# Attention and a bottleneck convolution on one core: the first output projection by quarters, weight parts prepared across the first batch, and three moved steps

## The chip, the cores and the metric

The kernel runs on one core of one Trainium2 chip. The metric is the device time of one execution in microseconds (us); lower is better. A profiled execution gives a span on the core, from its first to its last instruction, and a trace of every instruction on every engine.

## The reference, cut to what matters

Everything is float32. Four batches of a 1024 x 1024 token matrix pass through an attention layer and then a bottleneck convolution with batch norms over all four batches:

```python
B, C, H, W = hidden_states.shape          # 4, 1024, 32, 32
x = hidden_states.reshape(B, C, N).transpose(0, 2, 1)          # N = 1024 tokens
qkv = (x @ w_qkv.T + b_qkv).reshape(B, N, 3, nh, hd)            # 16 heads of 64
q, k, v = (qkv[:, :, 0], qkv[:, :, 1], qkv[:, :, 2])
q = _apply_rope(q, cos, sin); k = _apply_rope(k, cos, sin)
q = _rmsnorm(q.reshape(B, N, inner), q_norm_w); k = _rmsnorm(k..., k_norm_w)   # norm over all heads
attn = softmax(q k^T * hd ** -0.5)
out = _rmsnorm((attn v) @ w_proj.T, norm_out_w) + residual
...
out = relu(bn(conv1x1(x, w1)))            # 1024 -> 256 channels
out = relu(bn(conv3x3(out, w2)))          # 256 -> 256
out = bn(conv1x1(out, w3))                # 256 -> 1024
out = relu(x + softplus(residual_scale) * out)
```

## The kernel before, in words

**Stages.** The batches b = 0 to 3 are a Python loop (L958). Each has three projections, `q`, `k` and `v`, then attention in two halves c of the tokens with eight pairs of heads hp in each (`attention`, L753), then the output projection `y`. After the loop come the first convolution (`conv1`), the second (by tiles in a transformed domain, `uv`, L1166) and the third. All instructions of TensorE, VectorE, ScalarE and GpSimd (POOL) keep the order in which the Python code issues them; the loads on SyncE's queue (SP) are put in order by the framework.

**Projections by halves and by quarters.** A projection multiplies a 1024 x 1024 weight by 1024 x 1024 data with fewer products than the eight that the 2 x 2 blocks need. `project` (L290) does it *by halves*, one level: seven block products, each in four groups of output channels g, so 28 products of four matmuls of 512 columns. `project2` (L435) does it *by quarters*, two levels: seven outer parts k of seven products each, 49 products of four matmuls of 256 columns. The profile counts each float32 matmul as two instructions. Before the change batch 0 goes by halves and batches 1 to 3 by quarters.

**Weight parts.** By quarters, a weight of an outer part is needed as seven pieces: three are read as they are (m = 0, 1, 6), and four are sums that `prepare` (L400) makes once: four loads of 256 KB, four additions on VectorE (L407 to L410), four writes by POOL into the DRAM array `wd2` (L412). Such a group I call a *part*; there are seven per weight, 28 in all. Parts k = 2 to 5 are made from the one-level sums in `wd`, which batch 0's `project` makes itself in `operands` (L224: four loads, four additions L236 to L239, four writes L242, for each g). Where parts are made: in the attention of batch 0, one per pair of heads (`extra_step`, L989), the seven of q, the seven of v and one of k; in y of batch 0, by a delayed step (L1040), the other six of k; in the attention of batch 1 the seven of the output weight WP.

**Delayed steps.** `after(n, step)` (L254) puts a step n units later, a unit being one product by halves or two by quarters. `waiting` holds steps with a cost in units (`TT` per VectorE operation of 512 columns); `product_done` (L257) lets them out as the room allows. The rotation of q and k (`rope`, L699) is such a step for each of eight tiles: two VectorE operations of 1024 columns and two accumulating DMAs by POOL. After the last tile SP loads the tables of angles anew (`load_tables`, L168), which the norms had been multiplied into.

**Buffers.** Weights pass through a ring of eight 256 KB buffers (`wring`, L157), which parts made in attention use too. Parts in y of batch 0 use three larger ones (`big`). The tile of k and y (`kp`) and the room `v_room` are one buffer each, used in turn. PSUM has four banks `o1` and four `o2` during projections; the sums of a norm (`inverse_rms`, L674) take one of `o2`.

**Around y of batch 0.** The inverse denominators of the last pairs are computed at its start (`inverses`, L812) and copied by SP (L817, L822); `mean_of_v` (L747) multiplies by them and adds a bias on POOL (L751); the sums of data for the products (L281 to L284) follow.

**Around the second convolution.** `other_channels` (L1143) fills the padded tile of batch 0 (`fill`, L1097: a relu on ScalarE), VectorE makes differences of it (L1109), and then `fill(1, 1)` overwrites the tile with batch 1. `copies` (L1180) takes two banks from PSUM on ScalarE, after which TensorE goes on in them.

Of the kernel before, what the change touches and what calls it, by code (L numbers as in the profile page):

```python
# [11 lines left out]
F32 = mybir.dt.float32  # L12
AF = mybir.ActivationFunctionType
ALU = mybir.AluOpType
# [71 lines left out]
def program(ctx, tc, x, wblk, w2, w3, vecs, cos, sin, out, bad):  # L86
# [66 lines left out]
    with tc.tile_pool(name=f"st{u}", bufs=2) as st, ExitStack() as s:  # L153
# [14 lines left out]
        def load_tables():  # L168
            nc.sync.dma_start(cosT, cos)
            for i in range(2):  # L170

                nc.sync.dma_start(sinT[i::2, :], sin[1 - i :: 2, :])
# [25 lines left out]
        def bank(kind, name):  # L198
            pool, shape = psum[kind]
            return pool.tile(shape, F32, tag=kind, name=name)  # L200
# [43 lines left out]

        TT = 0.21
        later, waiting = [], deque()
        pace = {"at": 0, "room": 0.0, "hold": False}

        def spend(cost):
            pace["room"] -= cost
# [1 line left out]
        def after(n, step):  # L254
            later.append((pace["at"] + n, step))
# [144 lines left out]
        def prepare(which, base, k, alloc, queue=nc.sync):  # L400

            a11, a12, a21, a22 = a = alloc(f"pre_{which}_{k}")
            for i, t in enumerate(a):
                quarter(t, base, k, i // 2, i % 2, queue)

            def make():
                nc.vector.tensor_tensor(a22, a21, a22, ALU.add)  # L407
                nc.vector.tensor_tensor(a21, a11, a21, ALU.subtract)
                nc.vector.tensor_tensor(a11, a22, a11, ALU.subtract)
                nc.vector.tensor_tensor(a12, a12, a11, ALU.subtract)  # L410
                for m, t in enumerate((a11, a22, a21, a12)):
                    nc.gpsimd.dma_start(wd2[which, k, m], t)  # L412

            return make

# [246 lines left out]
        def beside(bs, ts, units, odd):  # L662


            def room(k):
                at = 8 + 4 * ((k + odd) % 2)
                return units[at : at + 4]

            def spare(k, oq, tq):
                return units[2 * (k % 2)] if (oq, tq) == (0, 1) else units[4 + 2 * oq]  # L670

            return operand(bs, ts), room, spare

        def inverse_rms(total, eps, scale, name, then):  # L674


            r = temp(f"rms_{name}")[:, :QT]
            row = inv_d[norms_done.pop(0)]

            def root():  # L680
                o = bank("o2", f"ss_{name}")[:, :QT]
                for q in range(4):
                    nc.tensor.matmul(
                        o[q * QH : (q + 1) * QH, :], ones[:, :QH], total[:, q * QT : (q + 1) * QT],
                        start=True, stop=True,
                    )
                nc.scalar.activation(r, o, AF.Sqrt, bias=eps, scale=scale)
                after(0.5, invert)

            def invert():  # L690
                spend(3 * TT)
                nc.vector.reciprocal(r, r)
                nc.gpsimd.dma_start(row.rearrange("(q t) -> q t", q=4), r[::QH, :])
                nc.gpsimd.dma_start(total, row.partition_broadcast(P))
                after(2.5, then)

            after(4, root)

        def rope(b, dst, total, eps, scale, w, tag, biased=True):  # L699

            def tables():
                for t in (sinT, cosT):
                    nc.vector.tensor_tensor(t, t, total, ALU.mult)

            def turn(f):
                k, other = dst[:, f, :], big_temp(f"{tag}s_{b}_{f}")
                for i, (t, table) in enumerate(((other, sinT), (k, cosT))):
                    if w is not None:  # L710
                        nc.vector.scalar_tensor_tensor(t, k, w[i][:, f : f + 1], table, ALU.mult, ALU.mult)
                    elif biased:
                        nc.vector.tensor_tensor(t, k, table, ALU.mult)
                    else:
                        nc.vector.scalar_tensor_tensor(t, k, col("bq", f), table, ALU.add, ALU.mult)
                for i in range(2):
                    nc.gpsimd.dma_start(dst[i::2, f, :], other[1 - i :: 2, :], accum_op=ALU.add)  # L717
                if f == NT - 1 and (b, tag) != (B - 1, "k"):
                    load_tables()

            def then():
                waiting.append((4 * TT, tables))
                for f in range(NT):
                    waiting.append((4 * TT, lambda f=f: turn(f)))

            inverse_rms(total, eps, scale, f"{tag}_{b}", then)
# [211 lines left out]
        def units_of(room):  # L938

            units = [flat(room[:, i // 2 : i // 2 + 1, :])[:, half[i % 2]] for i in range(16)]  # L940
            return [t.rearrange("p (q e) -> p q e", q=2) for t in units]

        vector_and_act = {mybir.EngineType.DVE, mybir.EngineType.Activation}
        regions = ExitStack()
        regions.enter_context(tc.manual_schedule(engines=vector_and_act))
# [12 lines left out]
        for b in range(B):  # L958
# [3 lines left out]
            if b > 0:  # L962
                two2 = [beside(xs[b], ts[b], units, odd) for odd in (1, 0)]
                two2.append(in_place(xs[b], ts[b], room, True))
                ahead.append(two2[1][:2])
            two = (0, *two2[0], b == 1) if b > 0 else None
            tq = qk_proj(b, WQ, xs[b], ts[b], "bq", q_all, "q", w1 if b == 0 else None, two, True)
            rope(b, q_all, tq, eps_q, HD / C, None, "q", b == 0)
            k_all = kp.tile([P, NT, N], F32, tag="k", name=f"k_{b}")
            if b > 0:  # L970
                ahead.append(two2[2][:2])
            two = (3, *two2[1], False) if b > 0 else None
            tk = qk_proj(b, WK, xs[b], ts[b], "bk", k_all, "k", None, two)
            rope(b, k_all, tk, eps_rms, 1.0 / C, (wqk_other, wqk), "k")
            v = room
# [4 lines left out]

            todo = []
            if b == 0:
                todo = [(which, base, k) for which, base in ((0, WQ), (1, WV)) for k in range(len(OUTER))]
                todo.append((3, WK, 0))
            elif b == 1:
                todo = [(2, WP, k) for k in range(len(OUTER))]
            made = []

            def extra_step():  # L989
                if made:  # L990
                    made.pop()()
                if todo:
                    made.append(prepare(*todo.pop(0), pieces))

            extra = [extra_step] * (len(todo) + 1) if todo else []
            if b == B - 1:
                extra = filters()
            if b > 0:
# [22 lines left out]
            if b + 1 < B:  # L1021
                xs[b + 1] = x_tile(b + 1)
                ts[b + 1] = t_tiles(b + 1)
                rows = (0, 1, 4, 5, 2, 3, 6, 7)
                for j in range(NT):

                    def load(b=b, i=rows[j]):
                        for c in range(NCH):
                            load_x(b + 1, c, (i,))

                    after(3 + 1.5 * j, load)
                for i in range(0, NH, 2):

                    def queue(b=b, i=i):
                        waiting.append((7 * TT, lambda: sums(ts[b + 1], xs[b + 1], i)))

                    after(3 + 1.5 * (2 * i + 3) + 2, queue)
                if b == 0:
                    for k in range(1, len(OUTER)):
                        after(5 * k - 4.5, lambda k=k: after(4, prepare(3, WK, k, big_pieces, nc.gpsimd)))  # L1040
            else:
                back = {1: x_tile(b + 1)}
                for i in range(NT):
                    after(8 + 1.5 * i, lambda i=i: read_back(1, (i,)))
            yt[b] = kp.tile([P, NT, N], F32, tag="k", name=f"y_{b}")
            two = None
            if b > 0:
                two = (2, *in_place(q_all, tc_, yt[b], False), True)
                if b + 1 < B:
                    ahead.append(beside(xs[b + 1], ts[b + 1], units_of(room), 1)[:2])  # L1050
            ty = qk_proj(b, WP, q_all, tc_, None, yt[b], "y", None, two)
            if b + 1 < B:
                o_norm(b, ty, yt[b])
# [89 lines left out]
        def other_channels():  # L1143
            norm1(1)
            fill(0, 1)
            for j in (1, 2, 0, 3):
                across(1, j)
                for r in range(2):
                    down(0, 1, r, j)
            for r in range(2, 4):  # L1150
                down(0, 1, r)
            fill(1, 1)

        for b in range(2):
            load_h1(b)
# [87 lines left out]
        for b in range(B):  # L1243
# [8 lines left out]
            for f in range(NPT):  # L1252
                for h in range(2):
                    if b > 0:
                        start_banks(b, f, h)
                        uv(b, f, h, 0, 0)
                    uv(b, f, h, 0, 1)
                    copies(b, f, h)
                    for i in range(NPT):
                        uv(b, f, h, 1, i)  # L1260
                    if due:
                        outputs(*due)
                    due = (b, f, h)
                    for step in steps[:4]:
                        step()
                    steps = steps[4:]
# [138 lines left out]
```

## Time and profile before

| | us |
|---|---|
| median of 3 runs (2730.69 to 2731.75) | 2731.07 |
| profiled execution | 2734.88 |
| its span | 2733.0 |
| TensorE (PE) busy | 2692.9 |
| VectorE (DVE) busy | 2091.9 |
| ScalarE (ACT) busy | 1081.1 |
| GpSimd (POOL) busy | 403.3 |

The page is that of the profiled execution, so parts of it add up to its own span of 2733.0 and not to the median. Matmuls are pipelined: the start of one group of them to the start of the next is the time that a group takes, while the "us" of a group has its drain in it. In lines of the timeline the first two numbers are the start and the duration, and a bracket at the end gives idle time ahead of the group and what ended it. Two numbers beside an engine in a table of windows are the busy time and the count of instructions.

### The profile page before, as it was taken

Reading aid. Unit: us, or ns where it says so; the run is one execution under the profiler, and the core shown is the slowest. Engines: PE = TensorE matmul, PEld = TensorE weight load, DVE = VectorE, ACT = ScalarE, POOL = GpSimd, SP = SyncE. Lnnn points to the kernel's source line nnn. Section 1 sums busy time; section 2 is a strip of 40 time slices with the busy share of each in tenths; the row PEclk is TensorE's granted clock in tenths of the full one; section 3 lists DMA queues with packets and bytes.
Section 4 is the critical chain, followed back from the end, with each engine's and each line's share of the span. In section 5 each row is a group of like instructions: output and inputs, shape, how many; then the busy total and the mean of one; then the engine's idle time right before and its main releaser. Section 6 shows DMA issues by size and latency. Waiting matters only on the chain.

```text
span 2733.0 us, 32908 instructions
## 1 busy us (share of the span) xinstructions
PE 2692.9 (99%) x11746; PEld 1652.8 (60%) x11746; DVE 2091.9 (77%) x2406; ACT 1081.1 (40%) x1494; POOL 403.3 (15%) x471
## 2 busy tenths in 40 slices
PE   9999999999999999999999999999999999999997
PEld 4449633347888433588886333888884335846843
DVE  4355599966788889888888877887888878646987
ACT  2221455413342555333343555233525653312266
POOL 1033022332011232100112100100112201000000
PEclk9999999999999999999999999999999999999999
DMA  5376255587668645356667410665687103662165
GB/s 208 105 189 185 89 156 158 179 276 251 189 181 216 139 122 156 117 168 220 178 191 186 89 24 16 200 195 183 181 238 148 25 23 125 198 240 85 62 221 211
DMA packets 238252, 432.05 MB, mean 158 GB/s; under 512 B 27072, under 2 KB 116464, under 8 KB 238080
## 3 DMA queue, kind: packets, MB, share of 16 engines
q1 hardware_dynamic: 202784, 312.30, 36.4%
q0 software_dynamic: 35296, 117.56, 16.7%
q8 instruction: 96, 1.57, 0.2%
q14 instruction: 76, 0.62, 0.1%
HBM read 295.22 MB, written 96.78 MB: 143 GB/s over the span
## 4 chain that ended last, share of the span: by engine, by line
PE 92%; DMA 3%; DVE 2%; ACT 2%; issue 0%; SPq 0%; POOL 0%; ACTq 0%; POOLq 0%; DVEq 0%
PE sc L770 17%; PE cx L787 16%; PE p_q L461 9%; PE p_y L461 9%; PE p_v L456 8%; PE p_k L461 7%; PE c L859 4%; PE c L1309 4%; PE pa_q L304 2%; PE pa_v L312 2%; PE pa_k L304 2%; PE c2x L1170 2%; PE c2y L1170 2%; DMA w_v<-wdf 2%; PE pa_y L304 2%; PE dn L808 1%
## 5 line engine op out<-in xcount | busy, mean ns | idle before, releaser
L781 DVE TENSOR_TENSOR den<-den,p 128x1024 f32<-128x1024 f32 x384 | 470.5, 1225 | 41.1 <-DVE den L781 0.9
L777 ACT ACTIVATE p<-sc 128x1024 f32<-128x1024 f32 x512 | 476.2, 1043 | 55.6 <-PE sc L770 55.6
L770 PE MATMUL sc<-q,k 64*128 64x512 f32 x2048 | 457.1, 596 | 3.0 <-DVE to L482 2.3
L770 PEld LDWEIGHTS sc<-q,k 64*128 64x128 f32 x2048 | 191.2, 186 | 266.8 <-issue 121.5
L787 PE MATMUL cx<-p,to 128*64 128x512 f32 x1536 | 340.2, 595 | 0.0
L787 PEld LDWEIGHTS cx<-p,to 128*64 128x64 f32 x1536 | 106.0, 137 | 228.3 <-issue 228.3
L751 POOL TENSOR_SCALAR q<-q,vec 128x512 f32<-128x512 f32 x64 | 130.7, 2049 | 524.6 <-DVE q L750 514.3
L792 ACT COPY q<-cx 128x512 f32<-128x512 f32 x64 | 37.6, 587 | 357.3 <-PE cx L787 357.3
L456 PE MATMUL p_v<-w_v,x 128*128 128x256 f32 x696 | 157.9, 379 | 1.9 <-DMA w_v<-wdf 1.9
L461 PE MATMUL p_y<-q,w_y 128*128 128x256 f32 x696 | 157.5, 380 | 0.0
L461 PE MATMUL p_k<-to,w_k 128*128 128x256 f32 x672 | 153.1, 381 | 2.3 <-ACT k L549 1.5
L461 PE MATMUL p_q<-to,w_q 128*128 128x256 f32 x672 | 152.5, 380 | 0.1
L456 PEld LDWEIGHTS p_v<-w_v,x 128*128 128x128 f32 x696 | 132.0, 190 | 21.0 <-DMA w_v<-wdf 3.1
L461 PEld LDWEIGHTS p_y<-q,w_y 128*128 128x128 f32 x696 | 131.8, 190 | 20.7 <-issue 2.5
L461 PEld LDWEIGHTS p_k<-to,w_k 128*128 128x128 f32 x672 | 126.7, 190 | 23.5 <-ACT to L549 2.8
L461 PEld LDWEIGHTS p_q<-to,w_q 128*128 128x128 f32 x672 | 127.2, 190 | 19.5 <-issue 1.6
L779 DVE TENSOR_TENSOR den<-p 128x1024 f32<-128x1024 f32 x64 | 76.5, 1196 | 76.6 <-ACT p L777 76.6
L814 DVE RECIPROCAL rec<-dn 128x512 f32<-128x512 f32 x32 | 107.2, 3350 | 14.1 <-PE dn L808 14.0
L787 PE MATMUL cx<-p,rq 128*64 128x512 f32 x512 | 113.4, 595 | 0.0
L1309 PE MATMUL c<-h,w 128*128 128x512 f32 x256 | 110.3, 592 | 0.9 <-ACT h L1213 0.9
L717 POOL DMA_DIRECT2D q<-qs x64 | 55.6, 1020 | 289.6 <-issue 190.8
L717 POOL DMA_DIRECT2D k<-ks x64 | 55.2, 997 | 242.1 <-ACT p L777 91.1
(521 smaller groups left out, 4271.9 us busy)
## 6 DMA issues: line engine op xcount, KB each, us to landing
wd2f<-w_pre POOLq DMA_DIRECT2D x88, 256.0 KB, 2.9
w_q<-wd2f SPq DMA_DIRECT2D x84, 256.0 KB
w_k<-wd2f SPq DMA_DIRECT2D x84, 256.0 KB
w_v<-wd2f SPq DMA_DIRECT2D x84, 256.0 KB
w_y<-wd2f SPq DMA_DIRECT2D x84, 256.0 KB
x<-in_x_dram SPq DMA_DIRECT2D x64, 256.0 KB
q<-qs POOLq DMA_DIRECT2D x64, 256.0 KB, 5.4
k<-ks POOLq DMA_DIRECT2D x64, 256.0 KB, 5.4
```

What stands on the lines that cost most here:

```text
L304: nc.tensor.matmul(o, w[:, i, :], r(i), start=first and i == 0, stop=last and i == NH - 1, skip_group_check=True,)
L456: nc.tensor.matmul(o[:, q].rearrange("p (g f) -> p g f", g=2), r[:, i, q * P : (q + 1) * P], wt[:, :, i, :], skip_group_check=True, **at,)
L461: nc.tensor.matmul(o[:, q], wt[:, q, i, :], r[:, i, :], skip_group_check=True, **at)
L717: nc.gpsimd.dma_start(dst[i::2, f, :], other[1 - i :: 2, :], accum_op=ALU.add)
L751: nc.gpsimd.tensor_scalar(cx, cx, col("bv", hp), None, ALU.add)
L770: nc.tensor.matmul(sc[:, j], k_all[d, hp, t * P : (t + 1) * P], q_all[d, hp, at], start=True, stop=bad is not None,)
L777: nc.scalar.activation(p, sc, AF.Exp)
L781: nc.vector.tensor_tensor(d_, d_, p, ALU.add)
L787: nc.tensor.matmul(o[j * HD : (j + 1) * HD, :], v[:, t, h0 : h0 + HD], probs[t][:, j], start=(t == 0), stop=(t == N // P - 1),)
L859: nc.tensor.matmul(o, w[f][ih][:, ii, :], ys[:, i, half[c]], start=(i == 0), stop=(i == NT - 1))
L1170: nc.tensor.matmul(o[:, r * TR * TC : (r + 1) * TR * TC], uw[2 * h + r, j][:, i * PL + f * P : i * PL + (f + 1) * P], vt[b, i][:, 2 * h + ...
L1309: nc.tensor.matmul(os[i], w3t[k][f // NH][:, f % NH, :], h2[b, k][:, half[c]], start=(k == 0), stop=(k == NPT - 1),)
```

## The change

Line numbers below are those of the kernel before.

- The output projection of batch 0 goes through `project2`, as those of later batches. Its one-level sums of WP are made by a new `prepare_blocks` in the attention of batch 0, and the sums ahead for q of batch 1 are made at its end.
- Parts are spread anew. Seven (three of q, three of v, one of k) are made in q of batch 0, in a tile of `kp` that k takes later; five (four of q, one of k) in k of batch 0, in `room`, which v takes later; both are loaded by POOL. In the attention of batch 0: four blocks of WP, its seven parts, and five of k, the loads of the first being issued ahead of the attention. Four of v are made in y of batch 0 (the last one ends in q of batch 1). None are left in the attention of batch 1.
- The rotation of k waits until 2.5 units after the tables of angles are loaded (`pace["tables"]`).
- The sums of the norms take a bank of `o1` rather than `o2`, but for q and k of batch 0.
- `TT` goes from 0.21 to 0.19.
- `fill(1, 1)` is issued after the first `copies`.

```diff
-        TT = 0.21
+        TT = 0.19
...
+        def prepare_blocks(base, g, alloc, queue=nc.sync):
+            a11, a12, a21, a22 = a = alloc(f"blk_{base}_{g}")
+            for i, t in enumerate(a):
+                ih = i % 2
+                queue.dma_start(t, wblk[base + g + NG * (i // 2)][:, ih * NH * P : (ih + 1) * NH * P])
+            def make():
+                nc.vector.tensor_tensor(a22, a21, a22, ALU.add)
+                nc.vector.tensor_tensor(a21, a11, a21, ALU.subtract)
+                nc.vector.tensor_tensor(a11, a22, a11, ALU.subtract)
+                nc.vector.tensor_tensor(a12, a12, a11, ALU.subtract)
+                for o, t in enumerate((a11, a22, a21, a12)):
+                    nc.gpsimd.dma_start(wd[base // NT * NG + g, o], t)
+            return make
...
-                o = bank("o2", f"ss_{name}")[:, :QT]
+                o = bank("o2" if name in ("q_0", "k_0") else "o1", f"ss_{name}")[:, :QT]
...
                     load_tables()
+                    pace["tables"] = pace["at"] + 2.5
...
             def then():
+                if pace["at"] < pace["tables"]:
+                    after(pace["tables"] - pace["at"], then)
+                    return
...
+        def weight_parts(parts, first, step, lag, alloc):
+            for i, (which, base, k) in enumerate(parts):
+                def begin(which=which, base=base, k=k):
+                    after(lag, prepare(which, base, k, alloc, nc.gpsimd))
+                after(first + i * step, begin)
...
-            two = (0, *two2[0], b == 1) if b > 0 else None
+            two = (0, *two2[0], False) if b > 0 else None
+            if b == 0:
+                unused = kp.tile([P, NT, N], F32, tag="k", name="unused")
+                parts = [(which, base, k) for which, base in ((0, WQ), (1, WV)) for k in (0, 1, 6)]
+                parts.append((3, WK, 0))
+                weight_parts(parts, 8, 2.7, 2.5, pieces_of(unused))
...
+            if b == 0:
+                parts = [(0, WQ, k) for k in (2, 3, 4, 5)] + [(3, WK, 1)]
+                weight_parts(parts, 2, 4.5, 2.5, pieces_of(room))
...
             if b == 0:
-                todo = [(which, base, k) for which, base in ((0, WQ), (1, WV)) for k in range(len(OUTER))]
-                todo.append((3, WK, 0))
-            elif b == 1:
-                todo = [(2, WP, k) for k in range(len(OUTER))]
+                todo = [lambda g=g: prepare_blocks(WP, g, pieces) for g in range(NG)]
+                todo += [
+                    lambda which=which, base=base, k=k: prepare(which, base, k, pieces)
+                    for which, base, ks in ((2, WP, (0, 1, 6, 2, 3, 4, 5)), (3, WK, (2, 3, 4, 5, 6)))
+                    for k in ks
+                ]
...
-                    for k in range(1, len(OUTER)):
-                        after(5 * k - 4.5, lambda k=k: after(4, prepare(3, WK, k, big_pieces, nc.gpsimd)))
+                    weight_parts([(1, WV, k) for k in (2, 3, 4, 5)], 6, 7, 4, big_pieces)
...
-            two = None
-            if b > 0:
-                two = (2, *in_place(q_all, tc_, yt[b], False), True)
-                if b + 1 < B:
-                    ahead.append(beside(xs[b + 1], ts[b + 1], units_of(room), 1)[:2])
+            two = (2, *in_place(q_all, tc_, yt[b], False), True)
+            if b + 1 < B:
+                ahead.append(beside(xs[b + 1], ts[b + 1], units_of(room), 1)[:2])
...
             for r in range(2, 4):
                 down(0, 1, r)
-            fill(1, 1)
...
                     copies(b, f, h)
+                    if (b, f, h) == (0, 0, 0):
+                        fill(1, 1)
```

`pieces_of(tile)` hands out quarters of a tile's sixteen 512-column pieces in turn; `extra_step` is called once ahead of the attention, so that the first loads are under way.

More of the change, by code (lines that the diff above doesn't have):

```diff
@@ L243, in operands @@
             return [a11, s1, a21, a12, a22]
-        TT = 0.21
+        TT = 0.19
         later, waiting = [], deque()
-        pace = {"at": 0, "room": 0.0, "hold": False}
+        pace = {"at": 0, "room": 0.0, "hold": False, "tables": 0.0}
         def spend(cost):
@@ L941, in units_of, with pieces_of, alloc @@
             return [t.rearrange("p (q e) -> p q e", q=2) for t in units]
+        def weight_parts(parts, first, step, lag, alloc):
[3 more added lines that the diff above has]
+                after(first + i * step, begin)
+        def pieces_of(tile):
+            at = deque(tile[:, i, h] for i in range(NT) for h in half)
+            def alloc(name):
+                at.rotate(-4)
+                return [at[i] for i in range(-4, 0)]
+            return alloc
         vector_and_act = {mybir.EngineType.DVE, mybir.EngineType.Activation}
@@ L992, in extra_step @@
                 if todo:
-                    made.append(prepare(*todo.pop(0), pieces))
-            extra = [extra_step] * (len(todo) + 1) if todo else []
+                    made.append(todo.pop(0)())
+            extra = [extra_step] * len(todo)
+            if todo:
+                extra_step()
             if b == B - 1:
```

## The prediction

> **What bounds the kernel now.** I read the busy times first, then the chain that ended last, then TensorE's waits, then the timelines of the stretches that the change touches.
>
> ```profile
> PE 2692.9 (99%) x11746; PEld 1652.8 (60%) x11746; DVE 2091.9 (77%) x2406; ACT 1081.1 (40%) x1494; POOL 403.3 (15%) x471
> PE 92%; DMA 3%; DVE 2%; ACT 2%; issue 0%; SPq 0%; POOL 0%; ACTq 0%; POOLq 0%; DVEq 0%
> ```
>
> TensorE is busy 99% and is 92% of the chain. Only fewer matmuls, or fewer waits of TensorE, can pay; work moved among the others costs nothing until TensorE waits for it. I call a projection by its letter and batch: q_0 is 5.4 to 103.8 us, k_0 to 200.7, v_0 to 301.7, the attention of batch 0 to 535.7, y_0 (output projection) to 639.4. Now TensorE in y_0, and after it the windows of q_0, k_0, y_0, y_1:
>
> ```profile
> 549.51 13.90 PE L304 MATMUL pb_y<-q,w_y 128*128 128x512 f32 x32
> 567.19 6.54 PE L304 MATMUL pa_y<-to,w_y_0b 128*128 128x512 f32 x8 [3.78 <-issue]
> 573.57 3.60 PE L304 MATMUL pc_y<-to,w_y_0b_s 128*128 128x512 f32 x8
> 577.00 3.60 PE L304 MATMUL pa_y<-q,w_y_0b 128*128 128x512 f32 x8
> ```
>
> ```profile
> 5.40:103.80 98.40, 98.37 (x225) 43.46 (x226) 37.92 (x62) 20.95 (x35) 8.56 (x16) 1.00 0.49 172
> 103.80:200.70 96.90, 96.90 (x234) 42.63 (x233) 51.08 (x61) 23.38 (x38) 23.97 (x34) 1.00 0.61 168
> 535.70:639.40 103.70, 99.59 (x228) 43.48 (x225) 63.67 (x81) 18.73 (x32) 43.46 (x66) 0.97 0.78 263
> 1133.50:1218.00 84.50, 84.50 (x391) 73.96 (x392) 75.09 (x93) 25.64 (x45) 6.34 (x4) 1.00 0.66 203
> ```
>
> (Columns: stretch, length, busy us of PE, PEld, DVE, ACT, POOL, clock, share of the DMA engines, GB/s.) A product by halves is 8 matmul instructions, 3.43 us apart. y_0 has 28: 96.1 us, but it takes 103.8, and one line shows where most of the 7.6 us go: 3.78 idle for late operands, then 6.54 us for a product instead of 3.60. y_1 is the same projection by quarters: 49 products at 1.727 us, 84.6 us, with no wait in it. Last, what y_0 starts behind (POOL writes a prepared part, SP loads weights), and the late wait in the convolution:
>
> ```profile
> 537.88 2.18 POOL L412 DMA_DIRECT2D wd2f<-w_pre  x4
> 540.32 3.85 SPq L221 DMA_DIRECT2D w_y<-in_wblk_dram  x4
> 543.84 7.46 DMA w_y<-in_wblk_dram
> 2499.46 1.25 ACT L1098 ACTIVATE pad<-h1l,sh,sc 128x1024 f32<-128x1024 f32 x1 [5.14 <-DVE cols L1109]
> 2501.22 1.83 PE L1170 MATMUL c2x<-V,t_w 128*128 128x256 f32 x4 [2.39 <-ACT c2x L1185]
> ```
>
> **What the Trainium skill says.** "TensorE: Matmul & The Clock Gate", Part 1: The HAM clock gate: after an idle window of about 3.4 us the array runs at half rate until it has been busy for about as long. The trace agrees: +2.9 us after 3.78 idle; and 2.39 idle at 2501 costs nearly as much (1.83 and 1.91 for runs of 1.03). So I price a TensorE wait of 2 us or more at itself plus 2 to 3. The same page, Architectural detail: VectorE is a strict FIFO. The trace agrees: from 545.5 to 552.4 VectorE sits before L750 for a DMA, and the first addition of pb_y, whose product ends at 553, comes at 563.8 behind it. "DMA: Bandwidth & Descriptors", Queues, rings and completion order: a DMA engine takes packets of its queues in turn. So parts loaded by POOL do not block SP's weights, but share the bandwidth; the trace shows 7.46 us for a 256 KB load at 543.84, where the parts' writes take 2.9.
>
> **The change part by part.** Durations are of the profiled execution, 2734.88 us with a span of 2733.0; it stands 3.8 above the median of 2731.07, and I take the difference off the median.
>
> (a) y_0 by quarters: 103.8 to 85.0 (y_1's stretch from first matmul to q_2's). **-18.8**: 11.5 is arithmetic, the rest y_0's present waits.
>
> (b) The new start of y_0. All weights pass through a ring of 8 buffers. The last part of the attention holds four; VectorE adds it up at 534 to 537.5, POOL writes it at 537.9 to 540.1, behind its two bias additions, and the buffers come free from 540.3 to 543.8, as SP's four w_y loads show. By halves the four buffers are wanted at 549.5 (A12). By quarters the fifth product (the start of the second of seven outer parts) is due at 535.7 + 4 x 1.727 = 542.6, and its weight is the eighth of the ring, fourth behind that release: issued at about 544.5, in about 4 us later, with 1 MB in the burst. TensorE waits about 5.5 and restarts at half rate, 2.5: **+8**, ends +2 (loads in 2 us, no half rate) and +12 (7.46 us again). Behind it on SP stand the x8 copies of the inverse denominators, so the last means of v and the second sums end near 558, as now (L282 at 557.6); they are wanted by the 14th product, 558.1 plus this wait. No second wait there.
>
> (c) The rest of y_0. VectorE as in y_1, 75.1, plus three of v's four parts at 4 x 0.69 = 2.8: 83.5 of some 94 us, and its first sums start 3 us later against TensorE than y_1's (537.5 for 535.7, 1131.8 for 1133.4). DMA: 17.2 MB as in y_1 plus three parts of 2.1 MB; at the 0.337 MB/us that y_0 has now (27.3 MB in 0.78 x 103.7) 74 of 94 us. Both fit, tightly: **+1.5**, ends 0 and +6.
>
> (d) k_0 gets five parts, q_0 seven, all loaded by POOL: per part 4 loads of 0.72 us on POOL, 4 additions on VectorE, 4 writes of 0.54. q_0: VectorE 37.9 + 19.6 = 57.5 of 98.4; DMA in 35 to 70 us 0.41 plus 3.6 parts at 6.2 us: full. But operands are done there 8 us before use (61.5 for 69.5): **+0.5**, ends 0 and +4. k_0 is the narrow one: from 132 to 166 VectorE is busy 29.8 of 34 us with q's rotation, DMA 0.83; two parts add 5.6 and 12.4. The operands of group 2 (L238) end at 161.3 now and are wanted at 166.4. The written order puts two parts and one more turn (2.4) before them and about 3 us of idle time is there to absorb it: 161.3 + 8 - 3 = 166.3, if no part is late. But POOL issues the second part's loads behind writes that wait for VectorE (about 151), 6 to 8 us before they land. Queued behind VectorE's wait are those operands, and SP's last piece of group 3 waits for the tables, thus for the turn: it is in at 179 now, wanted at 183.5. **+3**, ends 0 and +9.
>
> (e) Attention 0 has 16 parts for 15 (four are WP's operand sums, that y_0 made itself); attention 1 loses seven. 0: VectorE 210.6 + 2.8 of 233.4, and no wait of TensorE there names it or a DMA.
>
> (f) The relu (1.25 us) behind the copies: they no longer stand behind it and VectorE's columns (2499.4). TensorE's products end at 2498.8, so copy and go on at about 2499.6 instead of 2501.2: 1.6, and its slow restart (1.8): **-3.2**, ends -1 and -4.
>
> (g) TT, tables, banks: in the written order seven of q's turns, not five, precede k's norm in batches 1 to 3, and six of k's, not four, the attention. VectorE in a k stage rises from 70.3 to 75.5 of 86.8, y_1's share, which TensorE doesn't feel. Waits for w_v (6.0 in all) are table and weight loads meeting; they move rather than vanish. The norms' sums find free banks either way: no wait names one. **0**, ends -4 and +5.
>
> Sum: -18.8 + 8 + 1.5 + 0.5 + 3 - 3.2 = **-9.0**: 2722.1.
>
> **Rivals.** *The start is covered* (loads in 2 us, parts in time): -18.8 + 2 + 1 - 3.2 + 0.5 = -18.5, 2712.6. For it: the writes of parts take only 2.9 us. Against: SP's release at 543.8 comes after the due time of 542.6. *The gain is eaten*: y_0 waits as long as now (11), and 3, 6 and 1 in (c), k_0, q_0: -1, 2730. For it: the 7.46. Against: by halves the same moment also loads a part on POOL. *VectorE held by late parts in k_0, slower*: each part blocks it until POOL's loads land, behind writes that wait for VectorE in turn. It decides from 9.0 + 5.5 + 3 = 17.5 us, 3.5 of lost time for each of five parts; at 20 plus 3 in (c) the sum is +9.5, 2740.5. For it: the six parts that y_0 makes now held VectorE 17.9 us for their loads and 7.3 for a write. Against: that cost TensorE 0.34. *No change of matmuls* is excluded: the written order of TensorE has 49 products in y_0.
>
> **How the numbers follow.** Forecast 0.5, covered 0.20, eaten 0.18, slower 0.12. 0.2%, 5.5 us, is about what a measurement of this kernel tells from no change. Faster by more: 0.70; within: 0.18; slower: 0.12. The range reaches from just past the covered case to 2734, where only the slower case and the tail of the covered one are left out.
>
> **What would show it.** y_0 should be 90 to 99 us with one wait at its fifth product, for DMA w_y; k_0 97 to 106 with VectorE idle before L407 or L236; the c2x wait gone, q_0 below 103. A y_0 of 86, or a k_0 above 115, or waits for DVE scattered through y_0, would make the prediction wrong in (b), (d) or (c).

## The result, and the profile after

The changed kernel takes **2792.55 us** (median of 6 runs, 2783.1 to 2797.2) where the kernel before took 2731.41 in the same comparison: a ratio of 1.0218 (95% interval 1.020 to 1.0236). The profiled execution took 2791.24 us with a span of 2789.4, 56.4 more than the span before. First the busy times and the chain that ended last, after:

```profile
PE 2702.7 (97%) x11914; PEld 1695.5 (61%) x11914; DVE 2127.9 (76%) x2461; ACT 1089.0 (39%) x1507; POOL 428.9 (15%) x511
PE 81%; DVE 9%; DMA 6%; ACT 2%; issue 1%; SPq 0%; POOL 0%; DVEq 0%; POOLq 0%; ACTq 0%
```

TensorE's share of the chain fell from 92% to 81%, and VectorE, the DMAs and ScalarE have what it lost. The span grew by 56.4 us, yet TensorE is busy only 9.8 longer: it waits. TensorE's waits of the kernel after (in all, times, longest):

```profile
PE p_v L473 <- DMA w_v<-in_wblk_dram: 18.3, 5, 6.3
PE p_k L478 <- ACT to L566: 9.4, 6, 2.9
PE p_v L473 <- DMA w_v<-wdf: 8.4, 4, 3.2
PE pa_k L304 <- DVE w_k_2b L238: 6.1, 1, 6.1
PE p_v L473 <- DMA w_v<-wd2f: 5.9, 3, 4.8
...
PE p_q L478 <- ACT q L532: 4.6, 1, 4.6
...
PE p_y L478 <- DVE rec L835: 2.4, 1, 2.4
PE p_y L478 <- DMA w_y<-in_wblk_dram: 1.7, 1, 1.7
```

The waits of p_v for its weights are 32.6 us where they were 6.0, and products behind such waits run slowly: p_v<-w_v,x alone is busy 171.4 us for 157.9 before. The stages say where it went (us from a stage's first matmul to the next one's, from TensorE's timelines; e1, e4 and e14 are runs told below):

| stage | before | after | e1 | e4 | e14 |
|---|---|---|---|---|---|
| q_0 | 98.4 | 98.0 | 98.9 | 98.7 | 98.3 |
| k_0 | 96.9 | **106.0** | 109.8 | 105.4 | 99.4 |
| attention 0 | 233.3 | 233.3 | 233.3 | 233.3 | 233.5 |
| y_0 | 103.8 | **91.3** | 91.8 | 94.2 | 86.4 |
| q_1 | 85.6 | **91.9** | 91.9 | 92.8 | 86.9 |
| k_1, k_2, k_3 | 86.8 each | 92.9, 89.8, 89.8 | 90.7, 86.8, 86.8 | 92.4, 92.8, 91.5 | 86.8, 86.8, 86.9 |
| v_1, v_2, v_3 | 88.2, 89.3, 88.9 | **100.1, 100.1, 109.0** | 87.6, 86.7, 86.7 | 87.0, 88.6, 88.0 | 87.4, 86.5, 87.2 |
| second convolution | 116.6 | 114.3 | 114.3 | 114.3 | 114.3 |

What the change was aimed at did come: y_0 is 12.5 us shorter, the second convolution 2.3. The loss is elsewhere: 9.1 in k_0, 6.3 in q_1, 12.1 in k_1 to k_3 and **42.7 in v_1 to v_3**, stages whose matmuls the change doesn't touch.

Now the end of v_1 after, POOL and TensorE from the timelines:

```profile
880.40 1.74 POOL L734 DMA_DIRECT2D k<-ks  x2 [5.11 <-ACT to L553]
885.19 1.74 POOL L734 DMA_DIRECT2D k<-ks  x2 [3.05 <-ACT to L566]
886.29 6.61 POOL L1052 DMA_DIRECT2D x1df<-in_x_dram  x7
...
917.27 3.63 PE L473 MATMUL p_v<-w_v,x 128*128 128x256 f32 x8 [3.73 <-DMA w_v<-in_wblk_dram]
```

and the chain of waits there:

```profile
883.92 12.53 PE p_v L473 x58
896.45 0.02 issue
896.47 20.67 DMA w_v<-in_wblk_dram
917.13 0.14 issue
917.27 3.63 PE p_v L473 x8
```

The last piece of w_v, 256 KB issued at 896.5, is in after **20.7 us**. What else was on the way are the eight x1df transfers, 512 KB each, that add the input to the residual (L1052; L1000 before): POOL issues seven from 886.3 and the eighth at 893.3, in the middle of v's last weights, 65.5 us after v_1's first matmul. Before, POOL did it 94.8 us after v_1's first matmul, in the attention:

```profile
903.06 1.70 POOL L717 DMA_DIRECT2D k<-ks  x2 [23.57 <-ACT p L777]
905.58 1.70 POOL L717 DMA_DIRECT2D k<-ks  x2 [0.81 <-ACT p L777]
906.65 7.43 POOL L1000 DMA_DIRECT2D x1df<-in_x_dram  x8
```

They are issued in the program behind `rest(leave=4)`, which lets out k's turns (a turn is the rotation of one tile) until four are left. At TT = 0.21 the planner (`product_done`) had placed only two turns within v, so `rest` put two more behind v's last sums; POOL had to wait for VectorE to make these (903.06 and 905.58) before it came to x1df. At 0.19 six turns are placed within v, `rest` has nothing to add, and nothing on POOL stands between the sixth turn (885.19) and x1df. Two turns more, which I counted on VectorE alone, opened a gate on another queue.

### The profile page after: what moved, and what is told of

Its sections match the earlier page's. It is cut to its first block, busy times and chain, and to the rows that moved or that the text cites. A ratio compares the mean times of both kernels' runs of the same rounds, so it can differ in the third digit from the quotient of the medians.

```text
span 2789.4 us, 33400 instructions
## 1 busy us (share of the span) xinstructions
PE 2702.7 (97%) x11914; PEld 1695.5 (61%) x11914; DVE 2127.9 (76%) x2461; ACT 1089.0 (39%) x1507; POOL 428.9 (15%) x511
## 3 DMA queue, kind: packets, MB, share of 16 engines
q0 software_dynamic: 38496, 128.05, 17.4%
## 4 chain that ended last, share of the span: by engine, by line
PE 81%; DVE 9%; DMA 6%; ACT 2%; issue 1%; SPq 0%; POOL 0%; DVEq 0%; POOLq 0%; ACTq 0%
PE sc L791 16%; PE cx L808 16%; PE p_y L478 9%; PE p_q L478 9%; PE p_v L473 7%; PE c L880 4%; PE c L1359 4%; PE p_k L478 3%; PE pa_v L312 2%; PE pa_q L304 2%; PE c2x L1218 1%; DMA w_v<-in_wblk_dram 1%; PE c2y L1218 1%; DMA w_v<-wdf 1%; PE dn L829 1%
## 5 line engine op out<-in xcount | busy, mean ns | idle before, releaser
L808 PEld LDWEIGHTS cx<-p,to 128*64 128x64 f32 x1536 | 106.0, 137 | 228.3 <-issue 228.3
L478 PE MATMUL p_y<-q,w_y 128*128 128x256 f32 x928 | 210.7, 380 | 1.9 <-DMA w_y<-in_wblk_dram 1.7
L478 PEld LDWEIGHTS p_y<-q,w_y 128*128 128x128 f32 x928 | 175.3, 190 | 30.9 <-issue 6.3
L473 PE MATMUL p_v<-w_v,x 128*128 128x256 f32 x696 | 171.4, 402 | 20.4 <-DMA w_v<-wdf 8.4
L473 PEld LDWEIGHTS p_v<-w_v,x 128*128 128x128 f32 x696 | 140.5, 203 | 44.4 <-issue 21.7
L478 PE MATMUL p_y<-to,w_y 128*128 128x256 f32 x384 | 90.4, 380 | 0.8 <-DMA w_y<-wdf 0.7
```

Of the source, the lines that this page charges most:

```text
L473: nc.tensor.matmul(o[:, q].rearrange("p (g f) -> p g f", g=2), r[:, i, q * P : (q + 1) * P], wt[:, :, i, :], skip_group_check=True, **at,)
L478: nc.tensor.matmul(o[:, q], wt[:, q, i, :], r[:, i, :], skip_group_check=True, **at)
L808: nc.tensor.matmul(o[j * HD : (j + 1) * HD, :], v[:, t, h0 : h0 + HD], probs[t][:, j], start=(t == 0), stop=(t == N // P - 1),)
```

## The experiments

**e1 to e4: which part of (g).** Each takes one thing off the kernel after.

```
e1   -        TT = 0.19
     +        TT = 0.21
e2   -                    pace["tables"] = pace["at"] + 2.5
e3   -                o = bank("o2" if name in ("q_0", "k_0") else "o1", f"ss_{name}")[:, :QT]
     +                o = bank("o2", f"ss_{name}")[:, :QT]
e4   -            if b > 0:
     -                for f in range(NT):
     -                    nc.gpsimd.dma_start(x1d[f, ...], x[b - 1, ...], accum_op=ALU.add)
                  for c in range(NCH):
                      attention(b, c, q_all, k_all, v, probs_, late, ready, extra)
     +                if b > 0 and c == 0:
     +                    for f in range(NT):
     +                        nc.gpsimd.dma_start(x1d[f, ...], x[b - 1, ...], accum_op=ALU.add)
```

e1: 

> The kernel after with TT = 0.21 again, all else kept. Theory A (the cheaper turns let the planner do more of k's turns before the attention, so that on POOL the eight 512 KB x1df transfers follow them into the end of v, where they hold up the last weights of v): v_1 to v_3 go from 100, 100 and 109 us back to 88 to 90, k_2 and k_3 from 90 to 87, q_1 and k_1 lose some of their 6; about 2725 to 2735 us. Theory B (the later angle tables are what collides with w_v): v stays at 100 to 109, about 2785. Theory C (the norms' sums in the banks of o1 delay ScalarE and the products of q_1 and k): v back or not, but k_1 to k_3 keep their 3 to 6 us.

e2: 

> The kernel after without the tables' delay (k's multiplication of the tables is queued as soon as the inverse norm is there). Theory A: x1df still stands in v's end, 2785 to 2797 us. Theory B: v_1 to v_3 back to 88 to 90, about 2750. Theory C: no change.

e3: 

> The kernel after with all norms' sums in the o2 banks again; the written order of every engine is the same, only the bank differs. Theory C: the waits of p_k for ACT (9.4 us) and of p_q (4.6 us) go, with their slow restarts some 15 to 20 us, about 2775. Theories A and B: no change, 2785 to 2797.

e4: 

> The kernel after, with the eight x1df accumulating transfers of each later batch issued behind the first half of the attention (c = 0) instead of ahead of it; the sums of k and all pacing as in after. Theory A: v_1 to v_3 lose most of their excess of 12, 11 and 20 us, the k stages stay at 90 to 93: about 2750 to 2760. Theory B: no change, since the tables stay late: 2785 to 2797.

Measured: e1 **2737.43** (ratio to before 1.0023, 1.0015 to 1.003), e2 2787.76 (1.0198, 1.017 to 1.0225; v_1 to v_3 99.4, 98.5 and 106.1), e3 2795.4 (1.0232, 1.0209 to 1.0254), e4 **2751.51** (1.0069, 1.0052 to 1.0086). Theory A holds, B and C fall. In e4 POOL comes to k's sixth turn as early as in after, but x1df doesn't follow:

```profile
883.13 1.71 POOL L734 DMA_DIRECT2D k<-ks  x2 [5.14 <-ACT p_v L558]
887.91 1.71 POOL L734 DMA_DIRECT2D k<-ks  x2 [3.08 <-issue]
926.52 1.71 POOL L734 DMA_DIRECT2D k<-ks  x2 [36.89 <-ACT q L813]
```

and v_1 to v_3 take 87.0, 88.6 and 88.0 again. So 41 of the 61 us by which the kernel after is slower are the place of eight transfers in each of three batches (45.5 by the v stages; y_0, k_2 and k_3 came out 2.9, 3.0 and 1.7 longer in e4's profile). e1 gives back these and 2 to 3 us of each k stage, which e4 keeps. In e3, whose written order is that of after on every engine, the waits named `ACT to L566` (9.4) and `ACT q L532` (4.6) are the same to the tenth: the banks do nothing that these runs show. e2's runs (2777.2 to 2792.5) overlap with those of after: at most a few us for the tables.

Where the 3 us of a k stage come from is seen in k_1 of the kernel after:

```profile
798.49 4.63 DVE L518 TENSOR_TENSOR k<-k 128x1024 f32<-128x1024 f32 x4
802.02 0.72 ACT L624 ACTIVATE k<-k,vec 128x512 f32<-128x512 f32 x1 [2.90 <-DVE k L518]
807.61 0.57 ACT L566 COPY to<-p_k 128x512 f32<-128x512 f32 x1
808.23 8.73 PE L478 MATMUL p_k<-to,w_k 128*128 128x256 f32 x32 [2.88 <-ACT to L566]
```

VectorE comes to the block sums (L518) 70.6 us into the stage; before, the same sums began at 64.9, behind two turns less. ScalarE's biases and squares of the finished block wait for them, and the copy that frees TensorE's next bank stands behind these on ScalarE. VectorE, busy for 75.1 of 92.9 us, was not full; one sum with a due time was late.

**e9: TT alone, on the kernel before.** Its diff is e1's, reversed. 

> The kernel before with TT = 0.19 and nothing else. Theory A: the x1df transfers stand behind six of k's turns instead of four, thus in the end of v; v_1 to v_3 grow by 10 to 20 us each and k_1 to k_3 by 3: 2775 to 2785. Rival (it needs the parts or y_0 by quarters beside it): 2728 to 2736.

Measured: 2782.7 (1.0178, 1.0162 to 1.0193); v_1 to v_3 102.1, 100.9 and 101.9 (+13.9, +11.6, +13.0), k_1 to k_3 +3.0, +4.7, +4.9. One constant, 0.21 to 0.19, costs 51 us with nothing else changed.

**e5: the rest of the change without (g).** e1 to e3's edits together. 

> The kernel after without TT = 0.19, the tables' delay and the new banks: what is left is y_0 by quarters, the spread parts and the relu behind the copies. The prediction's sum for these is 2722. If the price of TT is the only one of the three that counts, it takes what TT = 0.21 alone took, 2737, with k_0 near 106 to 110, q_1 at 92 and y_0 at 91; if the tables' delay has a price or a gain of its own at this pace, it differs by 3 to 5 us in k_1 or v_1.

Measured: 2738.56 (1.0027, 1.0016 to 1.0038), equal to e1. So without the three edits that I had priced at nothing the change still was no gain: the parts cost in k_0 (109.8) and q_1 (91.9) what y_0 (91.1) and the convolution gave. The next runs, all with TT = 0.21, ask why.

**e10: the relu alone, on the kernel before.** 

> The kernel before with the relu of the padding issued behind the first copies of the second convolution, as after has it, and nothing else. The prediction's step (f): 3.2 us less in the second convolution, 2727 to 2728; after itself has it 2.3 us shorter, so 2729 if it is the relu alone and the rest of its wait stays with V.

```
-            fill(1, 1)
...
                     copies(b, f, h)
+                    if (b, f, h) == (0, 0, 0):
+                        fill(1, 1)
```

Measured: 2730.8 (0.9997, 0.9988 to 1.0005), not to be told from before by its time; in the profile the second convolution is 114.30, 2.3 less, as in after. The wait of 2.4 for the copy is gone, and waits for `V` take 1.4 of it.

**e6, e7, e8: parts moved.** e6 makes k_0's five parts in the attention of batch 0; e7 puts W_V's parts closer, so that the third is not at y_0's end; e8 does both and leaves the attention's last step empty.

```
e6, e8  -                parts = [(0, WQ, k) for k in (2, 3, 4, 5)] + [(3, WK, 1)]
        -                weight_parts(parts, 2, 4.5, 2.5, pieces_of(room))
        +                todo += [lambda ...: prepare(which, base, k, pieces) for which, base, k in [(0, WQ, k) for k in (2, 3, 4, 5)] + [(3, WK, 1)]]
        ...
e6      +                n = 2 if len(todo) > left[0] - 1 else 1
e8      +                n = 2 if len(todo) > left[0] - 2 else 1
        ...
e7, e8  -                    weight_parts([(1, WV, k) for k in (2, 3, 4, 5)], 6, 7, 4, big_pieces)
        +                    weight_parts([(1, WV, k) for k in (2, 3, 4, 5)], 6, 5.5, 4, big_pieces)
```

e6: 

> TT = 0.21 with the five parts of k_0 made in the attention of batch 0 instead (two parts in five of its sixteen steps). Theory K (POOL's late loads hold VectorE in k_0 ahead of the operands of groups 2 and 3): k_0 goes from 109.8 to 97 us, the attention stays within 1 us (VectorE 212 + 14 of 233), q_1 and y_0 as they are: 2724 to 2726. Rival: VectorE fills the attention, which grows by 5 us or more, or the waits of k_0 are q's rotation itself and stay: 2730 or more.

e7: 

> TT = 0.21 with the four parts of W_V in y_0 5.5 products apart instead of 7, so that the third is no longer the last thing on VectorE before y_0's closing additions. Theory Q (these 2.8 us stand ahead of the additions, whose squares stand ahead of q_1's first copy on ScalarE): the wait of p_q for ACT (4.6 us) goes, q_1 takes 85.7 to 87 instead of 91.9, y_0 within 1 us: 2731. Rival (the sums of batch 1 and the norm of y_0 hold VectorE there anyway): q_1 stays at 90 or more, 2736 to 2738.

e8: 

> TT = 0.21, k_0's five parts in the attention, W_V's parts 5.5 apart, and the attention's last step without a part, so that VectorE is free for y_0's first sums and the reciprocal 3.4 us earlier and the weights' ring too. If theories K and Q hold and the last part is what delays y_0's fourth and fifth products: k_0 97, q_1 86, y_0 87 to 89 (waits for rec 2.4 and for w_y 1.7 gone): 2714 to 2718. If y_0's start waits for weights whatever VectorE does: y_0 91, 2718 to 2721.

Measured: e6 2734.01 (1.0009, 1.0003 to 1.0016), e7 2737.49 (1.0028, 1.0017 to 1.0038), e8 2727.93 (0.999, 0.9981 to 0.9998). Theory K is right about k_0 (96.90, all 12.9 us back) and wrong about where the parts can go: the attention grew by 11.3, its sums over `den` (the softmax's denominators) late. Theory Q is right about q_1 (87.8) and y_0 paid it back (95.7 for 91.8). In e8 the waits for `rec` and for the first block of w_y are gone, as expected, but y_0 takes 90.9 and not 87 to 89: with W_V's parts closer, e7 and e8 have waits of y_0 for `DVE q L444` (1.9 and 1.4) that e6 has not. In q_1 of the kernel after the part is seen ahead of what y_0 still owes:

```profile
636.56 0.68 DVE L407 TENSOR_TENSOR pre<-pre 128x512 f32<-128x512 f32 x1
...
638.73 0.69 DVE L410 TENSOR_TENSOR pre<-pre 128x512 f32<-128x512 f32 x1
639.34 0.68 DVE L499 TENSOR_TENSOR q<-q,p_y 128x512 f32<-128x512 f32 x1
...
643.58 0.59 ACT L532 COPY q<-p_q 128x512 f32<-128x512 f32 x1 [8.27 <-DVE y L499]
644.21 5.37 PE L478 MATMUL p_q<-to,w_q 128*128 128x256 f32 x16 [4.59 <-ACT q L532]
```

In y_1 of the same kernel, without a part, the same chain ends with nothing to spare: there ScalarE's copy runs 1242.10 to 1242.69 and q_2's third product starts at 1242.73. So the part's four additions, 2.8 us, are most of the 4.59 that TensorE waits; e12, told below, has no part there and waits for 1.3.

**e11, e12: VectorE's total, or the order?** e11 spreads e6's parts so that no two steps of the attention hold more than three, and leaves the last step empty; e12 makes also one of W_V's at the end of v_0, so that none is due at y_0's end.

```
e11, e12  (e6's edit, but for its count of parts per step)
          +            load = deque([1] + [1] + [2 if i % 2 else 1 for i in range(2, 15)] + [0, 0])
e12       -                    weight_parts([(1, WV, k) for k in (2, 3, 4, 5)], 6, 7, 4, big_pieces)
          +                    weight_parts([(1, WV, k) for k in (3, 4)], 6, 7, 4, big_pieces)
          +                    weight_parts([(1, WV, 5)], 27, 7, 4, big_pieces)
          +            if b == 0:
          +                weight_parts([(1, WV, 2)], 22.5, 3, 2.5, big_pieces)
```

e11: 

> TT = 0.21, k_0's five parts in the attention of batch 0 as in the earlier run, but two parts only in every second step (5, 7, 9, 11, 13) and none in the last one, so that two steps hold 10.4 x 2 + 3 x 2.8 = 29.2 us of VectorE against 29.2 of TensorE. Theory V (what counts is how much of VectorE's work stands before the sums of den in one pair of steps): the attention grows by 0 to 3 us instead of 11, k_0 97, y_0 88 to 91: 2716 to 2723. Rival (VectorE's total in the attention is what is too much): the attention stays at 244, 2728 to 2731.

e12: 

> As the run before, and of W_V's four parts one is made at the end of v_0 and only three stay in y_0 and q_1, none of them near y_0's closing additions. Theory Q: besides the gain of the run before, q_1 takes 86 to 87 without y_0 growing: 5 us less than that run, 2711 to 2718. Rival (the norm of y_0 and batch 1's sums are enough to hold ScalarE there): equal to the run before.

Measured: e11 2732.08 (1.0001, 0.9993 to 1.001), e12 2727.78 (0.9986, 0.9979 to 0.9992). Theory V fell: the attention took 246.5 in both. TensorE's timeline of e11 shows the loss spread over five pairs of steps where e6 had it in two waits:

```profile
419.10 1.05 PE L829 MATMUL dn<-den,ones 128*32 128x512 f32 x4
421.59 1.05 PE L829 MATMUL dn<-den,ones 128*32 128x512 f32 x4 [1.44 <-DVE den L802]
...
450.75 1.05 PE L829 MATMUL dn<-den,ones 128*32 128x512 f32 x4
453.23 1.05 PE L829 MATMUL dn<-den,ones 128*32 128x512 f32 x4 [1.43 <-DVE den L802]
```

My sum of 29.2 against 29.2 used a mean over the whole attention, with its emptier first steps. In a full pair of the kernel after (420.0 to 449.2 us) VectorE is busy 27.49 of 29.2 us with two parts; a third makes it 30.3, and the pair of e11 takes 31.6. Theory Q held: q_1 86.9 for 91.6 in e11, with y_0 unchanged at 87.7 (88.0 in e11).

**e13, e14, e15: place.** VectorE idles in the last third of v_0 (5.4 of 36 us busy between 275 and 311 in the kernel after). All three runs have W_V's parts as in e12. e13 makes three of k_0's parts there and the other two in the attention, whose first two steps take two each. e14 puts none of the five into the attention: nine parts in q_0, one at k_0's start and one behind its last operands, two in v_0's tail with W_V's first, fifteen in the attention (the four blocks of WP count as parts here), none in its last step. e15 is e14 with the part of k_0's start in the attention's last step instead.

```
e13  +                weight_parts([(0, WQ, 2), (0, WQ, 3), (0, WQ, 4)], 21.5, 2, 2.5, pieces)
     +            load = deque([2, 2] + [1] * 14 + [0])
e14  -                parts.append((3, WK, 0))
     -                weight_parts(parts, 8, 2.7, 2.5, pieces_of(unused))
     +                parts += [(3, WK, k) for k in (0, 1, 6)]
     +                weight_parts(parts, 7, 2.3, 2.5, pieces_of(unused))
     ...
     -                weight_parts(parts, 2, 4.5, 2.5, pieces_of(room))
     +                weight_parts([(0, WQ, 2)], 0.5, 3, 2.5, pieces_of(room))
     +                weight_parts([(0, WQ, 3)], 21, 3, 4, pieces_of(room))
     ...
     +                weight_parts([(1, WV, 2)], 22.5, 3, 2.5, big_pieces)
     +                weight_parts([(0, WQ, 4), (0, WQ, 5)], 20.5, 2, 2.5, pieces)
     ...
     -                    for which, base, ks in ((2, WP, (0, 1, 6, 2, 3, 4, 5)), (3, WK, (2, 3, 4, 5, 6)))
     +                    for which, base, ks in ((2, WP, (0, 1, 6, 2, 3, 4, 5)), (3, WK, (2, 3, 4, 5)))
e15  -                weight_parts([(0, WQ, 2)], 0.5, 3, 2.5, pieces_of(room))
     +                    for which, base, ks in ((2, WP, ...), (3, WK, (2, 3, 4, 5)), (0, WQ, (2,)))
```

e13: 

> As the last run (TT = 0.21, W_V's first part at the end of v_0), but of k_0's five parts three are made in the last third of v_0 (from its product 21.5 on, in the ring of weights, which is empty then) and the two others ride on the attention's first two steps, ahead of which VectorE idles some 10 us each. If the place decides: k_0 97, v_0 102, the attention 233 to 236 instead of 246.5, y_0 88, q_1 87: 2714 to 2719. If VectorE's total in the first batch decides: the attention stays at 243 or more, or v_0 grows by as much, 2725 to 2729.

e14: 

> TT = 0.21; nine parts in q_0 (2.3 products apart) instead of seven, one at the very start of k_0 and one behind its last operand sums (product 21 on), two and W_V's first in the last third of v_0, fifteen in the attention with none in its last step, three of W_V in y_0 and q_1. If the price is one of place: q_0 98 to 99, k_0 97 to 99, v_0 102, the attention 233 to 235, y_0 88, q_1 87: 2714 to 2720. If every part costs TensorE 2 to 3 us in the first batch wherever it stands, the sum of q_0 to y_0 stays at 630 and more, 2726 to 2731.

e15: 

> As the run beside it, without the part at k_0's start, which is made in the attention's last step instead, as in the kernel after. If place decides: k_0 97, y_0 91, 2717 to 2722; 3 us more than the run beside it, or equal to it if that part costs k_0 as much. If not, 2726 to 2731.

Measured: e13 2730.46 (1.0, 0.9991 to 1.0008), e14 **2713.82** (0.9938, 0.9925 to 0.9952), e15 2718.36 (0.9949, 0.9936 to 0.9963). e13 missed mainly for one wait: v_0's third part ended only at 316 us, two of WP's operand sums stood in each of the first two steps, and the first `dn` (the matmuls that close the denominators) behind them waited 8.4 us; the attention took 245.1. Its last step kept a part, and y_0 took 91.6. In e14 the number of parts is the same and so is VectorE's work (2128.6 us busy; 2128.9 in e1, whose TT it has), and the time is 23.6 us less than e1's: place decides. TensorE's longest waits of e14 are

```profile
PE pa_q L304 <- DMA x<-in_x_dram: 5.5, 1, 5.5
PE p_v L473 <- DMA w_v<-wdf: 3.3, 5, 1.0
PE p_k L478 <- ACT k L566: 1.5, 3, 0.5
...
PE p_y L478 <- DMA w_y<-wdf: 1.4, 1, 1.4
PE pa_k L304 <- DVE w_k_3b L238: 1.4, 1, 1.4
```

y_0 takes 86.4. e14 is the fastest kernel of this study, 17.9 us ahead of the kernel before. e15's part in the last step costs y_0 6.3 us (92.7), and leaving it out of k_0 gives 2.5 back.

## Why the prediction was wrong, point by point

**(g), the failed step.** What failed is the price of TT, put at nothing. (g) as a whole stood at 0, ends -4 and +5; its three edits cost 54 us (after against e5), and TT alone accounts for it (e1, e9). The text saw that "six of k's, not four" turns precede the attention, and asked only what this does to VectorE. It did not go along POOL's order, where those turns are what x1df stood behind. It took the 6.0 us of waits for w_v for "table and weight loads meeting"; what those are is not shown, but e2 shows that the tables' delay is not what made them 32.6. The second half of (g), that a k stage at 75.5 of 86.8 us isn't felt, failed too, by 3 us a stage: the busy time came as foreseen (75.1 in k_1), and says nothing of the one sum that is due. That the banks are free either way held (e3).

Without (g) the sum still said -9.0, and e5 measured +7.3. The two large misses there are k_0, 12.9 for the 3 of (d), and q_1, 6.3 for which no term stood.

**(a)** was right: e14's y_0, with its start free, is 86.4, 17.4 less than before against 18.8 predicted.

**(b)** was right in its path; its wait was nearly right and its restart did not come. By TensorE's waits VectorE comes first: 2.39 us before the fourth product, for the reciprocal that frees a bank and stands behind the last part's four additions. Then come 1.70 before the fifth, for its weight:

```profile
543.09 0.68 DVE L407 TENSOR_TENSOR w_pre<-w_pre,w_pre 128x512 f32<-128x512 f32 x1
...
549.13 3.35 DVE L835 RECIPROCAL rec<-dn 128x512 f32<-128x512 f32 x1
...
552.53 1.99 PE L478 MATMUL p_y<-y,w_y 128*128 128x256 f32 x8 [2.39 <-DVE rec L835]
556.22 1.97 PE L478 MATMUL p_y<-q,w_y 128*128 128x256 f32 x8 [1.70 <-DMA w_y<-in_wblk_dram]
```

But the chain that ended last does not pass through the reciprocal. It is the one that (b) wrote down, from POOL's bias additions over its write of the last part to the weight of the fifth product:

```profile
545.12 0.70 POOL q L772
...
546.89 1.12 POOL wd2f L412 x2
548.01 2.89 DMA wd2f<-w_pre
550.92 0.38 SPq L398
551.39 4.70 DMA w_y<-in_wblk_dram
```

The weight is in at 556.1. Without the first wait TensorE would have been at the fifth product at 544.70 + 4 x 1.727 = 551.6 and would have waited there for 4.6 us (an estimate from these starts) where (b) said 5.5. The slow restart, put at 2.5, is what failed: the products behind the two waits take 1.99 and 1.97 for 1.89. With a third wait of 0.70 that makes 4.8 of the 6.4 us by which y_0 is longer than y_1 (91.3 and 84.9), where (b) and (c) said 9.5. Without a part in the attention's last step y_0 is 86 to 88 (e11, e12, e14; e8 is told above); e13 and e15, which have one there, are at 91.6 and 92.7.

**(c)** has no place for q_1. "Three of v's four parts" fall into y_0 in the plan, but VectorE comes to the third's additions 0.6 us into q_1, ahead of y_0's closing ones, and it is paid there: 6.3 us, of which e12 took out 4.7 against e11 by leaving none at y_0's end. (Its "74 of 94 us" of DMA is 70 by its own figures, 17.2 and three times 2.1 MB at 0.337 MB/us; nothing hangs on it.)

**(d)** was right in its mechanism, place and direction, and too small: +9.1 for "+3, ends 0 and +9", and 12.9 at TT = 0.21 (e1).

```profile
162.13 0.69 DVE L407 TENSOR_TENSOR rq<-rq 128x512 f32<-128x512 f32 x1 [6.38 <-DMA rq<-wdf]
...
172.49 5.69 PE L304 MATMUL pa_k<-t,w_k_2b 128*128 128x512 f32 x8 [6.06 <-DVE w_k_2b L238]
```

VectorE waits 6.4 us for a part's loads with the operands of group 2 behind it; the "if no part is late" of (d) was the assumption that failed. The DMA engines were full there (share 1.00 from 135 to 175 us). q_0 took seven parts for nothing, and in e14 nine.

**(e)** held: the attention is 233.33 in both. That it had no room for more was not asked, and e6 showed it.

**(f)** -2.3 for -3.2 (its terms, 1.6 and 1.8, add up to 3.4): the wait for the copy left, two for `V` came, 1.5 in all.

The chance given to slower, 0.12, was for one mechanism in k_0. That mechanism came with about half the 17.5 us at which it would decide; what made the kernel slower was none of the cases. In the eaten rival the "as long as now (11)" doesn't agree with the 7.6 us that the prediction read from y_0, and the 2.39 idle at 2501 that "costs nearly as much" as 2.9 costs 1.7 by the figures beside it.

## What to carry to other kernels

When a planner's price changes, walk every queue past the instructions that moved, above all the one that issues DMAs: what follows them there moves as well, and a large transfer that nobody waits for can still hold up the weights. VectorE, busy for 81% of k_1 and 94% of a pair of the attention, had free time only at certain places, so that the parts had no price of their own: up to the end of the attention they cost 13 us in e1's order and 2.6 in e14's. And where a gate holds by accident, as two late turns did here, make one on purpose, as e4 does.

## What the runs showed of the hardware

The size of the contention was not expected. The Trainium skill, "DMA: Bandwidth & Descriptors", Queues, rings and completion order, says that a DMA engine takes packets of its queues in turn; so 4 MB on POOL's queue should slow SP's loads while it lasts. The trace agrees in that they are slow (turns by packet are not to be seen in it), and gives the number: from 880 to 920 us in v_1 of the kernel after POOL's queue took 67.4% of the 16 engines' time and SP's 36.7%, and a 256 KB load took 20.67 us, where 7.46 was the slowest that the prediction had seen. POOL's queue moved 5.24 MB in that share and SP's 4.76: a megabyte of POOL's transfers, all of which add to what they write, held the engines 1.7 times as long as one of SP's. Two windows of the kernel after, the end of v_1 and the start of the attention (columns as in the prediction), show how little room v had and how much the attention:

```profile
880.00:920.00 40.00, 33.42 (x140) 27.96 (x139) 24.32 (x31) 7.73 (x12) 10.26 (x12) 0.92 1.04 251
920.00:960.00 40.00, 40.00 (x185) 14.92 (x185) 32.14 (x26) 23.49 (x26) 3.47 (x4) 0.99 0.32 78
```

In the kernel before, with the transfers in the attention, the share from 900 to 940 us is 0.91, and TensorE is busy for 39.93 of the 40 us.

The price of a restart varies more than I took it to: after 2.39 and 1.70 us of waiting in y_0 the products cost 0.1 more, after 2.88 in k_1 four products took 8.73 us (1.7 more than at 1.73 apart), after 4.59 in q_1 two took 5.37 (1.8 more than 3.62). The granted clock says the same: 1.00 from 552.5 to 555 us in y_0, 0.58 from 808.2 to 812 in k_1, 0.56 from 644.2 to 648 in q_1.

In part open: why k_1 took 3.9 us more than before in e1 and 0.9 in e5, which differ in the tables' delay and the norms' banks. The traces show where: VectorE waits 2.14 us for the broadcast of q's inverse norm in e1 and 0.81 in e5 (5.9 and 4.3 us to its landing), TensorE then 2.72 and 1.40, and three products behind that take 7.13 and 5.45. Why the broadcast was slower in e1 I did not try.
